# Three expert tiles of the first image beside the second image's routing

## The chip, the cores and the metric

The kernel runs on one core of a Trainium2 chip. Its metric is the device time of one execution in microseconds (us). TensorE (PE) does matmuls and transpositions, VectorE (DVE) and ScalarE (ACT) elementwise work, reductions and function tables, GpSimd (POOL) elementwise work and indirect DMA, SyncE (SP) issues DMAs. DMAs are issued from SP, ACT and POOL, each with a queue of its own.

## The reference, cut to what matters

Two images x of 128 channels and 56 x 56 pixels go through four layers, each added to its input after a group norm. This is what the change touches, and its neighbours:

```python
x = x + agent_attention(gn(x))
x = x + conv3x3(gn(x))
# layer 2: 784 tokens of 512 numbers per image (2x2 patches), 8 experts, best two per token
logits = xp @ router_w
topv, topi = top_k(softmax(logits), 2); topv = topv / sum(topv)
for e in range(8):
    val, g = split(xp @ w1[e], 2)           # 512 -> 2 x 1024
    out += gate[:, e:e+1] * ((val * sigmoid(g)) @ w2[e])    # 1024 -> 512
x = x + out
# layer 3: two mambas over the 56 pixels of each row, forward and backward, fused, layer norm
x = x + bidirectional_mamba(gn(x))
```

## The kernel before

All is float32, x stays in SBUF, and the layers follow one another.

**Attention** (`short_attention`) ends with a tail in an order written out by hand: the last attention block's closing steps are interleaved with image 0's convolution in eight parts (four groups, `left` and `right` of each), by the list `tail`, one entry ahead of each part. After the last part, ten small VectorE operations look at extremes that were gathered on the way (`bad`, `worst`), one TensorE product sums them over partitions (L871), and `wide` is set (L872): a branch at the kernel's end repeats everything with a slower attention if an exponential went out of range. The scope's memory is handed on after that.

**Convolution and routing.** `PatchExperts.route` runs image 1's convolution (a generator that yields after each of its groups) and, after its first group, `patches(0)`: group norm of image 0, tokens laid out as columns (`xq`), router products `l_ps` (L1098) and `s_ps` (L1108), the best two experts by small VectorE operations (`hots`), and the tokens turned to rows `xt` (L1142, L1144; four buffers) and written to DRAM `xd` by SP (L1145). After the convolution comes `patches(1)`, and then one routing of all 1568 tokens: products with ones and a triangle count tokens per expert (`tot`, `pre`), a scan over tokens and experts gives each token a slot, experts get as many 128-slot tiles as they need (`tiles`, `ends`), `whose` is the expert of each tile, and 28 products of one-hot masks (56 records, L1267) turn token-to-slot into slot-to-token: `inv`, copied to `whom` (token of each slot) and `share` (its gate). All of this comes in the order that the framework's scheduler picks from the program's order and its own estimate of when operands are ready.

**Experts** (`run`): 25 tiles always, and as many more as a branch (`Switch`) asks for; here 28 in all. A tile loads its expert's `w1` (4 MB, L1303) and `w2` (2 MB, L1308) on SP into two buffers each, POOL gathers 128 rows from `xd` by `whom` (L1281), TensorE transposes them (L1320), VectorE copies (`xs_c`), 16 products give `h_ps` (L1330, 32 records), ScalarE and VectorE gate them (L1333, L1334). `down` of the tile before follows: transpositions (L1343), copies, 8 products `o_ps` (L1351, 16 records), scaling, and a write to DRAM `os` on ACT's queue (L1354).

**MambaWeights** turns the mamba layer's weights: 27 loads on ACT's queue (16 of them the transposed `A`, L1498), scalings (L1471), 30 transpositions with a VectorE copy each (L141, L142) and four products (L1490). It stands after `route` in the program; its buffers are free from the end of attention, so the scheduler puts its loads at 914 to 937 us and its transpositions at 936 to 1005 us.

**Mambas** (`mamba_pair`): in fixed order. `arrive(b)` gathers and adds the expert rows of image b (`combine`, seven steps and a last one) and takes its group norm in three stages. The opening books the first block's forward way (`f`) and backward way (`b`) at steps -31 to -1 (`conv`, `silu`, `low`, `step`, `error`, `log`, `softplus`, `weigh`, `send_steps`); after each step a tuple says how many steps of image 1's `arrive` follow. `send_steps` of the first block's f copies `dtu` on SP and `dt` on ACT's queue, eight DMAs each (L1795). Then 448 units run, each a decay on ACT (L1807), a product on POOL (`dBu`, L1818) and a scan on VectorE (L1840).

Of the kernel before, what the change touches and what calls it, by code (L numbers as in the profile page):

```python
# [10 lines left out]
ALU = mybir.AluOpType  # L11
# [397 lines left out]
def short_attention(net, wide, conv):  # L409
# [20 lines left out]
    with ExitStack() as ctx:  # L430
# [337 lines left out]
        with tc.manual_schedule(engines={E.PE, E.Activation, E.DVE}):  # L768
# [55 lines left out]
            for f in fetches:  # L824
                if f:
                    f()

# [7 lines left out]
                [deviations],  # L835
# [15 lines left out]


            bad = net.small.tile([P, 4], F32, name="bad", tag="bad")
            nc.vector.memset(bad, 0.0)
            worst = net.small.tile([P, 4], F32, name="worst", tag="worst")
            aflat = asum.rearrange("t b k h -> t (b k h)")
            for n, (v, op, cmp, limit) in enumerate(
                (
                    (ends[:, 0].rearrange("p b k -> p (b k)"), ALU.max, ALU.is_gt, 1e20),
                    (ends[:, 1].rearrange("p b k -> p (b k)"), ALU.min, ALU.is_lt, 1e-30),  # L860
                    (aflat, ALU.max, ALU.is_gt, 1e30),
                    (aflat, ALU.min, ALU.is_lt, 1e-20),
                )
            ):
                size = v.shape[0]
                nc.vector.tensor_reduce(worst[:size, n : n + 1], v, AX.X, op)
                nc.vector.tensor_single_scalar(bad[:size, n : n + 1], worst[:size, n : n + 1], limit, cmp)
            total = net.small.tile([P, 1], F32, name="bad_sum", tag="bad_sum")
            nc.vector.tensor_reduce(total, bad, AX.X, ALU.add)
            w_ps = bank("w_ps")  # L870
            nc.tensor.matmul(w_ps[0:1, 0:1], full[:, 0:1], total, start=True, stop=True)  # L871
            nc.vector.tensor_single_scalar(wide, w_ps[0:1, 0:1], 0.5, ALU.is_gt)  # L872
# [130 lines left out]
TILES = 32  # L1003


class PatchExperts:

# [14 lines left out]
    def route(self, dram, wpool, conv):  # L1022
# [9 lines left out]
        with tc.tile_pool(name="l2_route", bufs=1) as one, tc.tile_pool(  # L1032
            name="l2_route_ps", bufs=2, space=PSUM
        ) as ps:
            self.fewest = -(-2 * toks // SLOTS)
            none = one.tile([SLOTS, 512], F32, name="none")
# [38 lines left out]
            nc.gpsimd.tensor_scalar(floor, count_to[:, :most], float(SLOTS), 0.0, ALU.mult, ALU.add)  # L1075

# [5 lines left out]
            per = nt // NB  # L1082

            def patches(b):
                if b == 0:
                    self.xq = wpool.tile([P, 4, 2 * self.hidden], F32, name="xq", tag="w1")
                xq = self.xq
                mr = net.group_norm(b, ps, "tr")
                for q in range(4):
                    net.normed(  # L1090
                        xq[:, q, b * tok : (b + 1) * tok].rearrange("c (h w) -> c h w", w=half), self.place(b, q), mr
                    )
                lq = one.tile([P, tok], F32, name="lq", tag="lq")
                size = tok // 2
                for i in range(2):
                    l_ps = ps.tile([P, 512], F32, name="l_ps", tag="tr")
                    for q in range(4):
                        nc.tensor.matmul(  # L1098
                            l_ps[32 * q : 32 * q + 32, :size],
                            rw[:, q, :],  # L1100
                            xq[:, q, b * tok + i * size : b * tok + (i + 1) * size],
                            start=True,
                            stop=True,
                        )
                    nc.scalar.copy(lq[:, i * size : (i + 1) * size], l_ps[:, :size])
                s_ps = ps.tile([P, 512], F32, name="s_ps", tag="tr")
# [32 lines left out]
                for t in range(b * per, (b + 1) * per):  # L1139
                    tp = ps.tile([P, 512], F32, name="xt_ps", tag="tr")  # L1140
                    for q in range(4):
                        nc.tensor.transpose(tp[:T, q * P : (q + 1) * P], xq[:, q, t * T : (t + 1) * T], net.ident)  # L1142
                    xt = one.tile([T, 512], F32, name="xt", tag="xt", bufs=4)
                    nc.scalar.copy(xt, tp[:T, :])  # L1144
                    nc.sync.dma_start(self.xd[t * T : (t + 1) * T, :], xt)  # L1145

            for _ in conv(0):
                pass
            for k, _ in enumerate(conv(1)):
                if k == 0:  # L1150
                    patches(0)
            patches(1)


            share = [one.tile([T, nt], F32, name=f"share{n}") for n in range(2)]
            nc.vector.tensor_sub(share[1], tops[1], tops[0])
            nc.scalar.activation(share[1], share[1], AF.Exp)
            nc.vector.tensor_scalar_add(share[0], share[1], 1.0)
            nc.vector.reciprocal(share[0], share[0])
            nc.vector.tensor_mul(share[1], share[1], share[0])  # L1160


            both = one.tile(shape, F32, name="both")
            nc.vector.tensor_add(both, hots[0], hots[1])
            flat = both.rearrange("t n e -> t (n e)")
            tot = ps.tile([P, 512], F32, name="tot", tag="tr")
            nc.tensor.matmul(tot[:, : nt * experts], every, flat, start=True, stop=True)
            pre = ps.tile([P, 512], F32, name="pre", tag="tr")
            nc.tensor.matmul(pre[:T, : nt * experts], before, flat, start=True, stop=True)
            by_e = one.tile([P, experts, nt], F32, name="by_e")  # L1170
            nc.vector.tensor_copy(by_e, tot[:, : nt * experts].rearrange("p (n e) -> p e n", e=experts))
            upto = one.tile([P, experts, nt], F32, name="upto")
            nc.vector.tensor_tensor_scan(
                upto.rearrange("p e n -> p (e n)"),
                step.rearrange("p e n -> p (e n)"),
                by_e.rearrange("p e n -> p (e n)"),
                0.0,
                ALU.mult,
                ALU.add,
            )  # L1180

            over = one.tile([P, experts, most], F32, name="over")
            nc.vector.tensor_tensor(
                over,
                upto[:, :, nt - 1 : nt].to_broadcast([P, experts, most]),
                floor.unsqueeze(1).to_broadcast([P, experts, most]),
                ALU.is_gt,
            )
            tiles = one.tile([P, experts], F32, name="tiles")
            nc.vector.tensor_reduce(tiles, over, AX.X, ALU.add)  # L1190
            ends = one.tile([P, experts], F32, name="ends")
            nc.vector.tensor_tensor_scan(ends, every_e(net, one, experts), tiles, 0.0, ALU.mult, ALU.add)

            more = keep.tile([1, 1], I32, name="more")
            nc.vector.tensor_scalar_add(more, ends[0:1, experts - 1 : experts], -float(self.fewest))
            self.more = more

            past = one.tile([P, TILES, experts], F32, name="past")
            nc.vector.tensor_tensor(
                past,  # L1200
                ends.unsqueeze(1).to_broadcast([P, TILES, experts]),
                count_to.unsqueeze(2).to_broadcast([P, TILES, experts]),
                ALU.is_le,
            )
            whose = one.tile([P, TILES], F32, name="whose")
            nc.vector.tensor_reduce(whose, past, AX.X, ALU.add)
            self.whose = keep.tile([P, TILES], I32, name="whose_i")
            nc.vector.tensor_scalar_min(self.whose, whose, float(experts - 1))

            nc.vector.tensor_sub(upto, upto, by_e)  # L1210
            start = one.tile([P, experts], F32, name="start")
            nc.vector.tensor_sub(start, ends, tiles)
            nc.vector.tensor_scalar_mul(start, start, float(SLOTS))
            slot = one.tile(shape, F32, name="slot")
            nc.vector.tensor_tensor(
                slot,
                pre[:T, : nt * experts].rearrange("t (n e) -> t n e", e=experts),
                upto[:T].rearrange("p e n -> p n e"),
                ALU.add,
            )  # L1220
            nc.vector.tensor_tensor(slot, slot, start[:T].unsqueeze(1).to_broadcast(shape), ALU.add)


            self.slots = []
            inv = ps.tile([P, 512], F32, name="inv", tag="tr")
            rooms = [
                wpool.tile([P, self.hidden // P, 512], F32, name="room0", tag="w2").rearrange("p j d -> p (j d)"),
# [62 lines left out]
    def run(self, wpool, work, ps):  # L1290
# [68 lines left out]
        for j in range(self.fewest):  # L1359
# [3 lines left out]
            if last is not None:  # L1363
                down(*last)
# [765 lines left out]
```

## Time and profile before

| what | us |
|---|---|
| median of 3 runs (3123.26 to 3127.08) | 3124.91 |
| the profiled execution | 3131.49 |
| its span | 3129.8 |
| attention and image 0's convolution end | 933.5 |
| image 1's convolution, TensorE | 938.5 to 982.8 |
| routing until the first expert rows are there | 982.8 to 1031.4 |
| experts, TensorE | 1031.4 to 1678.9 |
| opening of the mambas, until the first scan | 1678.9 to 1757.1 |
| mambas | 1757.1 to 3129.8 |

The profile is of one execution. TensorE is busy 2836.3 us of the span, VectorE 2229.0, ScalarE 1758.0, GpSimd 1495.6. Lines of the timeline read: start, duration, engine, line of the kernel, operation, output<-inputs, shapes, count, and in brackets the idle time before it with what released it. PE records of float32 products come in two per product.

### The profile page before, as it was taken

The numbers are of one execution on the slowest core, as the hardware profiler recorded it, in microseconds if no ns is written. First come the engines' busy times: TensorE is split into PE (matmuls) and PEld (weight loads), VectorE is DVE, ScalarE is ACT, GpSimd is POOL, SyncE is SP. The second block draws the span as 40 slices with busy tenths as digits, with TensorE's granted clock in tenths as the row PEclk, the third lists the DMA queues.
The fourth block names the chain that finished last, engine by engine and source line by source line (L and its number), as shares of the span: only waits on it lengthen the run. The fifth ranks groups of instructions, "written<-read, shape, count | busy, mean of one in ns | idle before, by whom it ended". The sixth has DMA issues, their size and how long they took to land. (4 is left out here: it accounts for less than half of the span.)

```text
span 3129.8 us, 34601 instructions
## 1 busy us (share of the span) xinstructions
PE 2836.3 (91%) x12964; PEld 1082.0 (35%) x12964; DVE 2229.0 (71%) x2033; ACT 1758.0 (56%) x2634; POOL 1495.6 (48%) x793
## 2 busy tenths in 40 slices
PE   7999999999988899999996789989899899899885
PEld 3333333332335444444443223333223333233321
DVE  5879999998886011111112689999999999999996
ACT  5778888887741011111110577776777776777764
POOL 3000100100521000000002589999999999999996
PEclk9999999999998899999997789999889998899987
DMA  1000000000011777777854553444434535444440
GB/s 54 1 1 1 1 1 1 1 1 1 1 38 53 311 308 302 301 310 292 319 194 161 104 110 77 93 92 102 90 84 86 114 81 107 90 85 91 93 101 8
DMA packets 133525, 333.64 MB, mean 107 GB/s; under 512 B 20228, under 2 KB 90724, under 8 KB 129748
## 3 DMA queue, kind: packets, MB, share of 16 engines
q1 hardware_dynamic: 111104, 303.96, 33.8%
q0 software_dynamic: 5136, 14.70, 1.4%
q10 hardware_dynamic: 17092, 12.53, 1.3%
q8 instruction: 106, 1.74, 0.2%
q14 instruction: 87, 0.71, 0.1%
HBM read 262.56 MB, written 17.20 MB: 89 GB/s over the span
## 5 line engine op out<-in xcount | busy, mean ns | idle before, releaser
L1818 POOL TENSOR_TENSOR dBu<-dtu,Bs 128x896 f32<-128x896 f32 x448 | 944.9, 2142 | 54.9 <-DVE h L1840 45.4
L1840 DVE TENSOR_TENSOR_SCAN h<-dA,dBu 128x896 f32<-128x896 f32 x448 | 879.1, 2007 | 51.3 <-ACT dA L1807 49.2
L620 ACT ACTIVATE ex<-sc 128x896 f32<-128x896 f32 (+1 forms) x700 | 602.6, 917 | 125.1 <-PE sc L617 113.8
L627 DVE TENSOR_TENSOR ex_sum<-ex_sum,ex 128x1792 f32<-128x1792 f32 (+1 forms) x238 | 492.5, 2069 | 35.3 <-ACT ex L620 21.3
L1860 PE MATMUL y<-h,both 128*64 128x448 f32 x1792 | 477.3, 635 | 13.7 <-POOL h L1846 12.6
L617 PE MATMUL sc<-q,k 32*128 32x448 f32 (+1 forms) x2800 | 403.8, 588 | 3.6 <-ACT ex L620 2.9
L1330 PE MATMUL h_ps<-w,xs_c 128*128 128x512 f32 x896 | 392.7, 596 | 11.8 <-issue 9.9
L1807 ACT ACTIVATE dA<-dt,f_A 128x448 f32<-128x448 f32 x448 | 284.4, 637 | 104.8 <-DVE h L1840 76.6
L635 PE MATMUL av<-ex,va 128*32 128x448 f32 (+1 forms) x2800 | 334.4, 552 | 0.1
L1849 DVE TENSOR_TENSOR h<-h,c_ps 128x1792 f32<-128x1792 f32 x154 | 311.3, 2022 | 26.8 <-PE c_ps L1828 12.3
L1334 DVE TENSOR_TENSOR he<-h_ps,sg 128x512 f32<-128x512 f32 x56 | 38.6, 691 | 397.7 <-PE h_ps L1330 374.9
L582 POOL TENSOR_TENSOR a_e<-a_e,a_inv 112x784 f32<-112x784 f32 x14 | 41.6, 2973 | 584.2 <-ACT ex L620 394.6
L1807 ACT ACTIVATE dA<-dt,b_A 128x448 f32<-128x448 f32 x448 | 283.7, 636 | 62.0 <-DVE h L1840 49.8
L1281 POOL DMA_INDIRECT xr<-xd,whom x28 | 28.0, 999 | 534.7 <-PE xr_ps L1320 494.7
L1846 POOL TENSOR_TENSOR h<-h,Cs 128x1792 f32<-128x1792 f32 x70 | 279.3, 3990 | 5.9 <-DVE h L1840 5.9
L1828 PE MATMUL c_ps<-low,ident 40*64 40x448 f32 x616 | 172.3, 640 | 91.5 <-DVE h L1849 69.3
L1330 PEld LDWEIGHTS h_ps<-w,xs_c 128*128 128x128 f32 x896 | 168.7, 191 | 220.3 <-issue 202.4
L1860 PEld LDWEIGHTS y<-h,both 128*64 128x64 f32 x1792 | 118.3, 152 | 320.6 <-issue 258.5
L617 PEld LDWEIGHTS sc<-q,k 32*128 32x128 f32 (+1 forms) x2800 | 137.9, 181 | 230.1 <-issue 132.5
L1351 PE MATMUL o_ps<-w,ht 128*128 128x512 f32 x448 | 198.7, 596 | 7.9 <-DMA w<-in_L_conv_w_dram 7.9
L1353 ACT ACTIVATE ot<-o_ps,share 128x512 f32<-128x512 f32 x28 | 19.2, 687 | 285.7 <-PE o_ps L1351 285.7
L1333 ACT ACTIVATE sg<-h_ps 128x512 f32<-128x512 f32 x56 | 33.4, 597 | 257.9 <-PE h_ps L1330 257.9
(333 smaller groups left out, 3067.5 us busy)
## 6 DMA issues: line engine op xcount, KB each, us to landing
w<-in_L_conv_w_dram SPq DMA_DIRECT2D x28, 4096.0 KB, 19.4
w<-in_L_conv_w_dram SPq DMA_DIRECT2D x28, 2048.0 KB, 10.2
Bs<-far SPq DMA_DIRECT2D x56, 896.0 KB, 10.7
dtu<-sp_u SPq DMA_DIRECT2D x108, 224.0 KB, 3.9
dt<-dt SPq DMA_DIRECT2D x108, 224.0 KB, 5.2
Cs<-far SPq DMA_DIRECT2D x140, 112.0 KB, 7.4
os<-ot ACTq DMA_DIRECT2D x28, 256.0 KB, 7.7
xd<-xt SPq DMA_DIRECT2D x14, 224.0 KB, 2.7
```

The lines of the kernel that those rows point to most:

```text
L617: nc.tensor.matmul(sc[:size, j, :BLK], self.m.k[rows, at : at + size], self.q[rows, :], start=True, stop=True)
L620: nc.scalar.activation(ex[:size, 2 * g : 2 * g + 2, :], sc[:size, :, :BLK], AF.Exp, scale=scale)
L627: nc.vector.tensor_add(self.total[g][:size], self.total[g][:size], ex[:size])
L635: nc.tensor.matmul(self.av[rows, :BLK], self.m.va[:size, i, rows], self.ex[i][:size, h, :], start=i == 0, stop=i == STEPS - 1,)
L1330: nc.tensor.matmul(h_ps, xc[:, q, :], w1[:, q, f0 : f0 + 512], start=q == 0, stop=q == 3)
L1351: nc.tensor.matmul(o_ps, ht[:, i, :], w2[:, i, :], start=i == 0, stop=i == nj - 1)
L1807: nc.scalar.activation(self.dA[u][:, r * BLK : (r + 1) * BLK], self.dt2[:, m, r, :], AF.Exp, scale=self.w.A[:, j, 2 * m + r : 2 * m + r + 1],)
L1818: nc.gpsimd.tensor_tensor(self.dBu[u], self.dtu2[:, m], self.B[:, j, :].unsqueeze(1).to_broadcast(shape), ALU.mult)
L1840: nc.vector.tensor_tensor_scan(hf, af, bf, 0.0, ALU.mult, ALU.add)
L1846: nc.gpsimd.tensor_tensor(h4, h4, c, ALU.mult)
L1849: nc.vector.tensor_tensor(h4, h4, c, ALU.mult)
L1860: nc.tensor.matmul(self.y[r * H : (r + 1) * H, m, :BLK], both, self.hc[j][:, m, r, :], start=False, stop=j == PAIRS - 1)
```

## The change

1. **Verdict.** The ten VectorE operations (`judge`) and the product with `wide` (`verdict`) become entries six and eight of the attention's `tail`.
2. **Early tiles.** After `patches(0)`, `first_tiles` routes image 0's tokens alone and numbers the tiles that its tokens fill entirely (`ALU.is_ge` on `full`); the first three, `EARLY`, get their own `whose_0`, `whom_0`, `share_0`. `ahead` issues their loads and gathers and keeps their TensorE work as a list of 21 stages. `patches(1)` and the routing of all tokens then run with TensorE and ScalarE in the order of the program, and `go(n)` puts n stages between their steps; while `held` is a list, the sigmoid with its multiplication is kept back until `patches(1)` is through. The global routing numbers the full tiles of image 0 first, over 2 x 8 ends in place of 8.
3. **Memory.** The pools of weights, work and PSUM are open from the convolution on. `xq` and the masks lie in `room`, which the mambas' weights take over afterwards; `xt` has two buffers in place of four; masks of one image at a time.
4. **MambaWeights** loads into a pool that opens after `route`, and its outputs lie in `room`.
5. **Opening.** The tuple changes, and the first block's `dt` DMAs go from ACT's queue to POOL's.

The core of the diff:

```diff
             tail = [
...
-                [deviations],
+                [deviations, judge],
+                [],
+                [verdict],
             ]
...
             def patches(b):
-                mr = net.group_norm(b, ps, "tr")
+                go = self.go if b == 1 else lambda n: None
+                got = []
+                go(2)
+                for stage in net.norm_stages(b, ps, "o", got.append):
+                    fetch = stage()
+                    if fetch:
+                        fetch()
+                        go(1)
+                mr = got[0]
...
                     nc.scalar.copy(lq[:, i * size : (i + 1) * size], l_ps[:, :size])
+                go(1)
...
-                    xt = one.tile([T, 512], F32, name="xt", tag="xt", bufs=4)
+                    xt = one.tile([T, 512], F32, name="xt", tag="xt", bufs=2)
                     nc.scalar.copy(xt, tp[:T, :])
                     nc.sync.dma_start(self.xd[t * T : (t + 1) * T, :], xt)
+                shares(some)
+                if b == 1:
+                    held, self.held = self.held, None
+                    for stage in held:
+                        stage()
+                    go(1)
...
             for k, _ in enumerate(conv(1)):
                 if k == 0:
                     patches(0)
-            patches(1)
+                    first_tiles()
+                    self.ahead()
+            with tc.manual_schedule(engines={mybir.EngineType.PE, mybir.EngineType.Activation}):
+                patches(1)
...
+                self.go(2)
...
+                for n in range(2):
+                    at_n = one.tile([T, nt], F32, name=f"at{n}")
+                    split(hots[n], slot, slice(0, nt), at_n)
...
+                    for b in range(NB):
+                        self.go((0, 2, 1, 1)[2 * n + b])
+                        turned(
...
+                self.go(len(self.stages))
...
         def expert(j):
-            return bass.ds(nc.sync.value_load(self.whose[0:1, j : j + 1], ...), 1)
+            whose = self.whose_0 if j < EARLY else self.whose
+            return bass.ds(nc.sync.value_load(whose[0:1, j : j + 1], ...), 1)
...
+        def ahead():
+            self.stages, self.held = [], []
+            for j in range(EARLY):
+                e = expert(j)
+                self.stages += step(j, e, up_weights(e), gather(j))
...
-        for j in range(self.fewest):
+        for j in range(EARLY, self.fewest):
...
-                for to, src, queue in (..., (self.dt2, self.dt, nc.sync if m is None else nc.scalar)):
+                for to, src, queue in (..., (self.dt2, self.dt, nc.sync if m is None else nc.gpsimd)):
...
-                for _ in range((0, 0, 0, 0, 2, 1, 2, 1, 2, 0, 0, 0, 0, 0, 1, 1, 1)[step - first] if step - first < 17 else 1):
+                for _ in range((0, 0, 0, 2, 0, 1, 1, 0, 1, 1, 1, 1, 0, 1, 1, 1)[step - first] if step - first < 16 else 1):
...
-                    experts.route(dram, wpool, convolved)
-                    wts = MambaWeights(net, one, nat, bank)
-                with tc.tile_pool(name="l2_work", bufs=2, reuse_waits="tile") as work, tc.tile_pool(
-                    name="l2_ps", bufs=2, space=PSUM
-                ) as ps:
-                    experts.run(wpool, work, ps)
+                    experts.begin(wpool, work, ps)
+                    room = one.tile([P, 4 * experts.tok], F32, name="room", tag="room")
+                    experts.route(dram, work, ps, room, convolved)
+                    with tc.tile_pool(name="l3_nat", bufs=2) as nat:
+                        wts = MambaWeights(net, one, nat, bank)
+                    experts.run()
```

`step` is `up` and the `down` of the tile before it as a list of stages: the transposition, four half products (each pair followed by its gating), the transposition of `down`, two halves of its product. The 21 stages are those of tile 0 (5), tile 1 (8) and tile 2 (8). In order, `patches(1)` runs six of them, two follow the slots, four lie between the masks, and nine come after the last product of `inv`.

## Prediction

> **What bounds the kernel now.** I read the table of stages first. Attention (to 894 us) and the mambas (from 1757 us) are touched only at their ends, so the middle decides. There TensorE is nearly idle-free while experts run, and half starved before them:
>
> ```profile
> 982.80:1031.36 48.56, 30.68 (x159) 24.05 (x157) 28.37 (x113) 6.14 (x14) 5.46 (x6) 0.68 0.44 166
> ```
> ```profile
> 1094.80:1117.35 22.55, 22.16 (x61) 10.37 (x60) 2.67 (x4) 2.47 (x4) 0.99 (x1) 1.00 0.77 302
> ```
>
> After the stage and its length the columns are busy time of PE, PEld, DVE, ACT and POOL, granted clock, DMA share and GB/s. One expert tile takes 22.55 us, 22.16 of them TensorE's: nothing but TensorE work removed or filled in shortens that stage. The routing stage ahead of it has 48.6 us with 30.7 busy at clock 0.68. The timeline shows the serial end of it:
>
> ```profile
> 1011.26 12.18 PE L1267 MATMUL inv<-room 112*128 112x64 f32 x56 [5.18 <-DVE tile_f L1242]
> ...
> 1023.48 0.19 DVE L1276 CAST whom<-inv 128x32 int32<-128x32 f32 x1 [8.46 <-PE inv L1267]
> ...
> 1023.96 1.14 POOL L1281 DMA_INDIRECT xr<-xd,whom  x1 [39.06 <-DVE share L1278]
> ...
> 1031.36 0.88 PE L1320 MATMUL xr_ps<-ident,xr 128*128 128x128 f32 x3 [7.92 <-DMA xr<-xd,whom]
> ```
> ```profile
> 1094.81 0.60 PE L1320 MATMUL xr_ps<-ident,xr 128*128 128x128 f32 x4
> ```
>
> No expert can start before `whom` (1023.5) and its gather (1031.4). Tile 3, the first that the changed kernel runs in the old way, starts its transposes at 1094.81. The size of the middle's gain is how much earlier that row comes. The page's DMA issues bear on the rivals:
>
> ```profile
> w<-in_L_conv_w_dram SPq DMA_DIRECT2D x28, 4096.0 KB, 19.4
> w<-in_L_conv_w_dram SPq DMA_DIRECT2D x28, 2048.0 KB, 10.2
> ```
>
> In steady state SP issues the 2 MB and 0.6 us later the 4 MB; they land after 10.2 and 19.4 us, so the second one moves in the 9.8 us after the first: on SP's queue a transfer waits for what was issued before it.
>
> **Part 1, verdict.** Judge and verdict move into the attention's tail. Now the next stage waits for them:
>
> ```profile
> 935.68 0.15 DVE L872 TENSOR_SCALAR wide<-w_ps 1x1 int32<-1x1 f32 x1 [0.37 <-PE w_ps L871]
> 935.76 0.12 POOL L933 MEMSET scratch<- 128x16 f32 x1 [3.35 <-PE w_ps L871]
> ```
>
> The last statistics end at 933.5, the first plane is normalized at 935.92: **-2.4 us**. The ten small DVE operations (1.9 us) then lie beside conv matmuls that run to 929.8; without that cover they cost at most their 1.9.
>
> **Part 2, three tiles beside the routing.** TensorE is the bound from the end of image 1's conv (982.8) on, so I add up its work until tile 3.
> Start: 982.8 - 2.4. `first_tiles` puts 28 small matmuls into the conv stream, which is packed (13.73 us of conv records without a gap up to 982.8). The 56 like them took 12.18 us, 0.217 each, at granted clock 0.50; the projection of 112 columns (L674) ran at 0.13 each at clock 1.00. Bounds 3.6 and 6.1; I take 3.6, since TensorE is warm there. Conv ends at 984.0.
> Work: three tiles, 67.7; routing of image 1: l_ps 3.6, s_ps 1.6, xt 4.2, totals and norms 1.5, inv 56 x 0.13 = 7.3 (bound 12.2). Sum 18.2. Without a wait tile 3 starts at 984.0 + 67.7 + 18.2 = 1069.9, 25 us earlier than now.
> Waits: (a) tile 0's transposes stand ahead of image 1's norm in TensorE's order and need `whom_0`. Image 0's choice is made at 966.8; the chain from there to the last mask takes 13.6 us now (1001.4 to 1015.0); with image 0 alone its masks halve, but conv's DVE work stands between, so 13.6 stays, plus 1.5 for the last products: 981.9. Issue 1.1 and 7.3 us to land (the row above) give 990.3, less the 2.4 of part 1: 987.9. TensorE waits 3.9. (b) The copy `xs_c` after a transposition is uncovered for two tiles: 2. (c) `xt` has 2 buffers instead of 4. A write of it lands in 2.7 us and its copy takes 0.6, so the seven go in pairs of 3.3: about 3 late. ScalarE's held sigmoids stand behind these copies, with a table load of 1.28, and tile 1's products need the banks that they free: 3 more, 6 together. (d) `inv` waits for masks: 2. Sum 13.9.
> Tile 3 at 1083.8 instead of 1094.8: **-11.0 us, part 1 included**. Bounds: -25 (no wait) and +12 (the queue of the second rival, with the upper bounds of the small products).
>
> **Part 3, the mambas' weights** move behind the routing, into the stage where TensorE has 0.4 us free per tile. 30 transpositions at 0.15 (four take 0.60 at L1320) and 8 records of L1490 at 0.19 are 6.0 us, with no cover any more; their DVE work (50 operations of 0.28) has it, 2.7 of 22.55 being busy. Their 27 loads, 0.3 to 0.8 us of issuing each on ACT's queue, and two Exp now share ACT's order and the DMA engines with the experts (ACT is busy 2.5 of 22.55). Where they stand now they cost nothing that comes back: ACT's conv copies wait for them 5.5 and 3.1 us, but the conv records behind run packed. In the idle queues each 2 KB load of `A` landed in 2.3 us; beside weights I take 2 us of waiting (bounds 0 and 25). **+8.0 us.**
> The Trainium skill (DMA: Bandwidth & Descriptors, "Rules for kernel authors") speaks against the place: a strided last dimension becomes one descriptor per element, and its section on queues says that an engine alternates between queues at packet boundaries. By that the 16 `A` loads are 8192 descriptors that take turns with 32 KB ones, and the wait would lie near the upper bound, 25, and the sum at +14. No row of before has such loads beside weights.
>
> **Part 4, the opening.** The first scan now starts behind a chain:
>
> ```profile
> 1747.90 8.01 PE L1690 MATMUL conv_ps<-pad,b_conv_t 128*128 128x448 f32 x16
> ...
> 1750.23 0.64 ACT L1807 ACTIVATE dA<-dt,f_A 128x448 f32<-128x448 f32 x1 [3.60 <-DMA dtu<-sp_u]
> ...
> 1755.75 0.28 PE L116 MATMUL gn_ps<-gn_q,group 128*128 128x1 f32 x2
> ...
> 1756.26 0.20 ACT L67 ACTIVATE ir_t<-ir_v 128x1 f32<-128x1 f32 x1 [5.39 <-DVE ir_v L66]
> 1756.37 0.62 ACT L1807 ACTIVATE dA<-dt,f_A 128x448 f32<-128x448 f32 x1
> ...
> 1757.09 2.02 DVE L1840 TENSOR_TENSOR_SCAN h<-dA,dBu 128x896 f32<-128x896 f32 x1 [0.86 <-ACT dA L1807]
> ```
>
> The second half of the first decay stands on ACT behind image 1's root, this behind a product that TensorE runs after 8.0 us of conv. In the new order the root's product comes one step ahead of that conv, so this wait goes: the decay could end at 1751.5. What is late next is dBu on POOL (1750.58 + 2.13). POOL now issues eight `dt` transfers first, 0.8 each by its one direct issue (L1043): the four ahead of each memset push dBu to about 1753. Against that `step` no longer waits for two more combines (1730.97 would be 1728.2), -2.8, and ACT loses 2.6 us of issuing ahead of the second softplus. First scan at 1750 to 1751; way b's silu with its two table loads still stands between the first decays, so I take **-6 us**, bounds 0 and -10. From there on POOL is busy 478 and DVE 468 of every 500 us, so the shift stays to the end.
> The skill's first-byte figures (same page, "Latency and other measured facts") give POOL's queue 0.4 us more per transfer. The sum with that would be 0.4 higher.
>
> **Sum.** -11.0 + 8.0 - 6 = -9.0. The profiled execution took 3131.49 (span 3129.8), 6.6 above the median of the runs: applied to it 3122.5, to the median 3124.9 - 9.0 = **3116 us**. 0.2%, 6.2 us, is about what a measurement of this kernel can tell from no change.
>
> **Rivals.**
> *The waits fit.* The go() quotas cover waits (a) to (d) by half and the loads by luck of order: -7 and -2 more, -18: 3107. For it: ACT is busy 6.1 and DVE 28.4 of that stage's 48.6 us, and TensorE's clock stays up. Against it: its order is fixed, so one late operand stops all.
> *The queue on SP (slower).* Tile 0's 6 MB are issued as soon as `whose_0` is read, at about 971 (966.8 and the 4.2 us that `whose_i` now takes from 1001.4 to 1005.6). With two `xt` buffers the last writes of image 0's rows leave at about 975. If they stand behind, they land at 971.5 + 9.8 + 10.2 = 991.5, the gather at 1000 instead of 990: +9. The same again when tile 2's 4 MB, freed by tile 0's last product, go ahead of image 1's seven writes: the third copy waits up to 9.8 instead of 2.7, +7. Together +16: +7, 3132. It decides once it costs more than 9.0; above 15.2 it shows as slower.
> *The loads stop an engine.* An Exp of `A`, or a transposition of way b, stands in its engine's order and its bytes crawl behind weights: 10 to 20 more, +1 to +11, 3131. TensorE then idles between tiles 3 and 6.
> *It doesn't overlap.* Tile 0 comes so late that the routing simply starts after it; this is the queue's case with the same price and is counted there.
>
> **Numbers.** Forecast 0.44, waits fit 0.16, queue 0.22, loads 0.18. Faster: most of the first (0.38), all of the second, 0.01 of the loads: 0.55. Slower: 0.17 of the queue, 0.11 of the loads: 0.28. Same: the rest, 0.17. The forecast's own range is 3109 to 3122. The range over the cases goes down to the fitted waits with all loads hidden, 3100, and up to queue and loads in part together, 3139.
>
> **What would show it.** Right: `wide` written before the last conv statistics; xr_ps of tile 0 at 985 to 992; tile 3's at 1078 to 1089; transpositions L141 between experts with gaps under 1 us; first scan 70 to 74 us after the last expert product. Wrong: SP's xd writes landing after more than 8 us (queue); TensorE idle for over 5 us between experts before the Switch with ACT or a DMA as releaser (loads); a first scan still 78 us after that product (1678.9 to 1757.1 now).

## The result and the profile after

The changed kernel runs in 3123.76 us (median of 20), the kernel before, beside it on the same chip, in 3123.67 (median of 20). One run of the changed kernel was slow, 4028.81 us at a granted clock of 0.64, and is left out of the ratio of the mean times, 0.9994, 95% interval [0.9987, 1.0002]: -1.9 us, between -4.1 and +0.6. No difference can be told. The forecast was -9.0.

The two profiled executions (spans 3129.8 and 3125.7) can't be subtracted as they stand. Attention, which the change leaves alone but for its tail, ends 3.19 us earlier in the second (last `y_ps` at 901.88 and 898.69), 2.4 of it there already at 60 us. So I count from the end of that product:

| us from the end of attention's last y_ps | before | changed | difference |
|---|---|---|---|
| image 1's convolution starts | 36.63 | 36.08 | -0.6 |
| image 1's convolution ends | 80.92 | 85.91 | +5.0 |
| tile 0, xr_ps | 129.48 | 91.26 | -38.2 |
| tile 3, xr_ps | 192.93 | 190.70 | -2.2 |
| tile 4, xr_ps | 215.48 | 217.97 | +2.5 |
| last expert product ends | 777.01 | 780.01 | +3.0 |
| first scan | 855.21 | 854.07 | -1.1 |

Tile 0 starts 38 us earlier, and three tiles later nearly all of that is gone. The timeline of the changed kernel shows the start (PE's line names the gather that it waited for) and then the stretch in which it is lost:

```profile
989.95 1.11 PE L1465 MATMUL xr_ps<-ident,xr 128*128 128x128 f32 x4 [5.35 <-DMA xr<-xd,whom]
```
```profile
1010.64 0.33 SPq L1443 DMA_DIRECT2D w<-in_L_conv_w_dram  x1
...
1012.42 1.07 ACT L1165 COPY xt<-xt_ps 112x512 f32<-112x512 f32 x2 [4.92 <-PE xt_ps L1163]
...
1013.03 18.18 SPq L1166 DMA_DIRECT2D xd<-xt  x7
...
1014.92 0.28 DVE L1330 TENSOR_TENSOR both<-hot,hot 112x112 f32<-112x112 f32 x1
1024.39 1.15 ACT L1165 COPY xt<-xt_ps 112x512 f32<-112x512 f32 x2 [10.91 <-DMA xd<-xt]
...
1025.03 1.96 PE L1163 MATMUL xt_ps<-ident,room 128*112 128x128 f32 x8 [10.84 <-ACT xt L1165]
...
1028.90 1.06 PE L1465 MATMUL xr_ps<-ident,xr 128*128 128x128 f32 x4
...
1035.07 1.22 PE L1475 MATMUL h_ps<-w,xs_c 128*128 128x512 f32 x1 [3.44 <-DVE he L1484]
```

Read it from the bottom of the wait. TensorE stands 10.84 us for ACT's copy `xt`; ACT stands 10.91 for a write of `xd`, since two buffers are full; and the writes were issued at 1013.03, 2.4 us behind tile 2's `w1` of 4 MB. VectorE has chosen the experts by 1015.2 and waits too. Behind it tile 1's products wait 3.44 us for gates that were held back.

The table of stages (length, busy PE, PEld, DVE, ACT, POOL, granted clock, DMA share, GB/s), from the end of the convolution to the transposes of tile 1, from these to those of tile 2 and of tile 3, then tile 3 and tile 4:

```profile
984.60:1028.90 44.30, 26.07 (x100) 14.05 (x100) 9.29 (x31) 5.12 (x11) 3.29 (x4) 0.79 0.84 324
1028.90:1065.76 36.86, 32.86 (x122) 18.97 (x121) 21.37 (x74) 4.85 (x8) 2.22 (x3) 0.84 0.19 53
1065.76:1089.39 23.63, 22.55 (x63) 10.50 (x62) 2.67 (x4) 2.36 (x4) 1.85 (x2) 1.00 0.83 312
1089.39:1116.66 27.27, 27.27 (x99) 13.56 (x98) 12.12 (x46) 2.47 (x4) 1.00 (x1) 1.00 0.64 251
1116.66:1139.20 22.54, 22.15 (x61) 10.36 (x60) 2.67 (x4) 2.47 (x4) 1.00 (x1) 1.00 0.76 303
```

TensorE is idle for 18 of 44 us in the first. In tile 3's stage, with the mambas' weights in it, it is busy all the time, and the stage is 4.7 us longer than tile 4's (27.27 against 22.54). The attention's tail and the opening:

```profile
928.83 0.13 DVE L853 TENSOR_SCALAR wide<-w_ps 1x1 int32<-1x1 f32 x1
```
```profile
1738.97 7.85 SPq L1995 DMA_DIRECT2D dtu<-sp_u  x8
...
1743.61 0.16 DVE L66 TENSOR_SCALAR ir_v<-gn_ps 128x1 f32<-128x1 f32 x1 [0.54 <-PE gn_ps L116]
1743.81 0.20 ACT L67 ACTIVATE ir_t<-ir_v 128x1 f32<-128x1 f32 x1 [2.79 <-DVE ir_v L66]
...
1749.50 0.64 ACT L2007 ACTIVATE dA<-dt,f_A 128x448 f32<-128x448 f32 x1 [5.25 <-DMA dt<-dt]
...
1750.66 2.07 POOL L2018 TENSOR_TENSOR dBu<-dtu,Bs 128x896 f32<-128x896 f32 x1 [6.35 <-DMA dtu<-sp_u]
...
1752.76 2.02 DVE L2040 TENSOR_TENSOR_SCAN h<-dA,dBu 128x896 f32<-128x896 f32 x1 [7.68 <-POOL dBu L2018]
```

`wide` no longer stands between the layers, and ACT takes image 1's root at 1743.81, ahead of the decays. They now wait for the `dt` transfers, and the scan waits longer, for `dBu`, which POOL starts when the `dtu` copies have landed. Counted from the last expert product, these copies are issued 4.2 us sooner than in the kernel before (60.28 against 64.44), and yet `dBu` starts no sooner (71.96 against 71.69).

### The profile page after: what moved, and what is told of

It reads as the page before. It is cut to its first block, busy times and chain, and to the rows that moved or that the text cites. A ratio compares the mean times of both kernels' runs of the same rounds, so it can differ in the third digit from the quotient of the medians.

```text
span 3125.7 us, 34650 instructions
## 1 busy us (share of the span) xinstructions
PE 2831.0 (91%) x12996; PEld 1075.4 (34%) x12996; DVE 2242.2 (72%) x2096; ACT 1758.6 (56%) x2635; POOL 1492.7 (48%) x804
## 5 line engine op out<-in xcount | busy, mean ns | idle before, releaser
L2060 PE MATMUL y<-h,weights 128*64 128x448 f32 x1792 | 472.9, 629 | 11.9 <-POOL h L2046 10.8
L1475 PE MATMUL h_ps<-w,xs_c 128*128 128x512 f32 x896 | 400.1, 602 | 16.1 <-issue 9.9
L2060 PEld LDWEIGHTS y<-h,weights 128*64 128x64 f32 x1792 | 117.1, 151 | 318.5 <-issue 252.8
L1890 PE MATMUL conv_ps<-pad,weights 128*128 128x448 f32 x448 | 185.3, 561 | 3.6 <-issue 2.4
## 6 DMA issues: line engine op xcount, KB each, us to landing
w<-in_L_conv_w_dram SPq DMA_DIRECT2D x28, 2048.0 KB, 10.4
```

What stands on the lines that cost most here:

```text
L1475: nc.tensor.matmul(has["h"][:, n, :], has["xc"][:, q, :], w1[:, q, f0 : f0 + 512], start=q == 0, stop=q == 3)
L2060: nc.tensor.matmul(self.y[r * H : (r + 1) * H, m, :BLK], both, self.hc[j][:, m, r, :], start=False, stop=j == PAIRS - 1)
```

## The experiments

My first theory was the prediction's rival, in its second half: the writes of image 1's rows stand behind `w1` on SP's queue. Its rivals were the two buffers as such, a gain that is lost again in the expert stage, and a whole that is only the opening's. Line numbers in profiles of variants are their own.

**The writes on POOL's queue (e1_writes_pool).**

```diff
-                    nc.sync.dma_start(self.xd[t * T : (t + 1) * T, :], xt)
+                    (nc.gpsimd if b else nc.sync).dma_start(self.xd[t * T : (t + 1) * T, :], xt)
```

> The changed kernel with one line edited: the seven writes of the second image's rows (xd<-xt) are issued by POOL instead of SP; the first image's stay on SP. Theory (the queue on SP): in the changed kernel TensorE stood 10.84 us at 1025.03 because these writes were issued behind tile 2's 4 MB w1 (1010.64) and only two xt buffers exist. Away from SP's queue a write lands in about 2.5 us, so the xt copies run in pairs of some 3.5 us: tile 1's xr_ps moves from 1028.9 to about 1021.5, tile 3's from 1089.4 to 1082, and the whole by -6 to -8 us against the changed kernel, 0.9970 to 0.9977 of the kernel before. Rival A (the two buffers alone, whatever the queue): the wait stays over 7 us, tile 1 not before 1026, time within 2 us of the changed kernel (0.999). Rival B (the time goes further back, into the expert stage and the Switch): tile 3 comes 7 us earlier, but the last expert product stays within 2 us of 1678.7.

3131.12 us, 1.0015 of the kernel before [1.0003, 1.0027]. The wait is the same on another queue:

```profile
1017.62 0.33 SPq L1443 DMA_DIRECT2D w<-in_L_conv_w_dram  x1
...
1020.28 1.19 POOL L1166 DMA_DIRECT2D xd<-xt  x2 [24.87 <-ACT xt L1165]
1031.50 1.15 ACT L1165 COPY xt<-xt_ps 112x512 f32<-112x512 f32 x2 [11.03 <-DMA xd<-xt]
...
1032.14 1.95 PE L1163 MATMUL xt_ps<-ident,room 128*112 128x128 f32 x8 [10.96 <-ACT xt L1165]
```

10.96 instead of 10.84: that another queue would free the writes was wrong. The packets in the trace tell why, and that there are two mechanisms with one price:

| | w1's 128 packets of 32 KB | first two writes' packets |
|---|---|---|
| changed kernel (SP's queue) | 1011.61 to 1023.38 | all from 1022.60 on, when an engine's share of w1 is through |
| e1 (POOL's queue) | 1018.60 to 1031.05 | from 1024.13 to 1031.61, among them, about one for one |

A 32 KB packet takes 1.21 us, one of the writes 0.08 to 0.16. The Trainium skill (DMA: Bandwidth & Descriptors, "Rules for kernel authors") says that spreading DMAs over SP, ACT and GpSimd does not help bandwidth, since all run on the same engines and interleave; this run agrees, and shows that it does not help a small write's wait either.

Tile 1 comes 39.67 us after tile 0 instead of 38.95, and the last expert product ends at 779.97, as in the changed kernel (780.01). The rest of the +6 is elsewhere: the profiled execution ended attention 7.5 us later, with a granted clock of 0.73 between 160 and 185 us (1.00 in the changed kernel's), and its first scan comes 76.8 behind the last expert product instead of 74.1 (77.2 in e9 below, which writes from POOL too). That part is not explained.

**w1 later in the program (e2_w1_late).** Tile 2's `up_weights` and `down_weights` called behind the loop of writes.

> The changed kernel with tile 2's two weight loads (w1, w2) requested in the program's order behind the seven writes of the second image's rows, instead of ahead; all stay on SP's queue, with two xt buffers. Theory (the queue on SP): the same gain as with the writes on POOL, tile 1's xr_ps at about 1021.5, tile 3's at 1082, -6 to -8 us against the changed kernel; w1 then leaves at about 1020 instead of 1010.6, lands 20 us later, at 1040, ahead of its use at about 1058, so nothing is lost. Rival A (two buffers alone): no change, within 2 us. Rival C (the late load costs what the early writes win): tile 1 early, but tile 2's first h_ps waits for w1, and tile 3 stays at 1087 to 1091.

3125.41 us, 0.9998 [0.9986, 1.0011]. The edit did not do what it says: SP's order is the scheduler's, and it issued `w1` at 1014.50, after two of the writes. Those landed at once (a wait of 1.90 us), the other five stood behind `w1`, and the wait moved: 13.52 us, ended at 1031.01. A hint for the theory, no test of it.

**The opening alone, and all but the opening (e3_opening_alone, e4_no_opening).**

```diff
-for _ in range((0, 0, 0, 0, 2, 1, 2, 1, 2, 0, 0, 0, 0, 0, 1, 1, 1)[step - first] if step - first < 17 else 1):
+for _ in range((0, 0, 0, 2, 0, 1, 1, 0, 1, 1, 1, 1, 0, 1, 1, 1)[step - first] if step - first < 16 else 1):
...
-(self.dt2, self.dt, nc.sync if m is None else nc.scalar)
+(self.dt2, self.dt, nc.sync if m is None else nc.gpsimd)
```

e3 is the kernel before with this, e4 the changed kernel without it.

> The kernel before with part 4 alone: the new tuple that spreads the second image's arrival over the opening's steps, and the split dt transfers on POOL instead of ACT. Theory (the opening is what is left of the change): last expert product unmoved at 1678.9 within 0.3, first scan 74 us after it instead of 78.2, whole -4 us, 0.9987 of the kernel before (interval 0.998 to 0.9995). Rival (the opening's gain in the changed kernel comes from the earlier parts, such as weights already turned or room in memory): first scan still 77 to 78 us after the last expert product, time within 1 us of before.

> The changed kernel without part 4: the tuple and the queue of the dt transfers as in the kernel before, the early tiles, the verdict and the moved weights kept. Theory: parts 1 to 3 together are worth nothing at the end: tile 3's xr_ps at 1089.4, tile 4's at 1116.7, last expert product at 1678.7, first scan 78 us after it at 1757, and the time that of the kernel before, ratio 0.9990 to 1.0010. Rival (the early tiles give something that shows only at the end): 0.9985 or less, with a first scan before 1755. Rival (they cost and the opening hides it): over 1.0010.

e3: 3120.36 us, 0.9980 [0.9968, 0.9991]; first scan 73.61 behind the last expert product (78.20 before). e4: 3132.30 us, 1.0012 [1.0002, 1.0022]; 77.29, and the last expert product at 780.52 against 777.01. So the opening gives 6 us (3 to 10), parts 1 to 3 together cost 4 (1 to 7), and the changed kernel is their sum (-2.5 by these two, -1.9 measured). That e4 would be even was wrong, though its interval begins near even. The rows agree: the last expert product ends at 779.7 to 780.6 in the six profiles that have the early tiles, two buffers and `w1` ahead of most writes (changed, e1, e2, e4, e9, e10), at 777.0 and 776.6 without early tiles (before, e3). The even time is two effects that cancel.

**The verdict alone (e5_verdict_alone).** The kernel before with part 1.

> The kernel before with part 1 alone (judge and verdict inside the attention's tail). One look at the rows, counted from the end of the attention's last y_ps product, since the attention itself ends 1 to 4 us earlier or later from run to run. Before: conv of the second image ends 80.92 behind it, tile 3's xr_ps 192.93; changed kernel: 85.91 and 190.70. Forecast's theory: part 1 is worth 2.4 us or more, conv ends at 78.5, tile 3 at 190.5. Rival (what looked like -3.85 is the attention's own shift): the first normalized plane moves from 34.04 to about 33.4 and conv ends at 80.3, -0.7; then first_tiles puts 5.7 us into the conv stream of the changed kernel, not 3.6.

In the one profiled run image 1's convolution starts at 34.47 (before 36.63; 37.03 in e3, which has that stage too) and ends at 79.47 (80.92), tile 3 at 191.72 (192.93). The verdict is worth 2.2 to 2.6 us where it stands and 1.2 at tile 3. In the changed kernel only 0.6 is left at the start, as VectorE reaches `bad_sum` late there and TensorE waits for it:

```profile
925.82 0.19 PE L852 MATMUL w_ps<-bad_sum,full 128*1 128x1 f32 x2 [0.93 <-DVE bad_sum L847]
```

Loads and a scaling of `A` stand in its way: counted from the last `y_ps`, ACT takes the root of image 1's norm at 23.02 in the changed kernel, right behind an `A` load, and at 22.03 in e5; VectorE then has a scaling of `A` (1.03 us) ahead of the last check, and `bad_sum` comes at 26.92 instead of 25.52.

**w1 strictly behind the writes (e6_w1_behind), four buffers (e7_xt4), both (e8_w1_behind_xt4).**

```diff
-with tc.manual_schedule(engines={mybir.EngineType.PE, mybir.EngineType.Activation}):
+with tc.manual_schedule(engines={mybir.EngineType.PE, mybir.EngineType.Activation, mybir.EngineType.SP}):
...
                 shares(some)
                 if b == 1:
+                    self.late_w1()
```
```diff
-                    xt = one.tile([T, 512], F32, name="xt", tag="xt", bufs=2)
+                    if t % 2 and b:
+                        xt = work.tile([SLOTS, 512], F32, name="xt", tag="ot")[:T, :]
+                    else:
+                        xt = one.tile([T, 512], F32, name="xt", tag="xt", bufs=2)
```

`late_w1` requests tile 2's two loads, which `ahead` then leaves out. e6 is the first, e7 the second, e8 both.

> The changed kernel, tile 2's w1 and w2 loads requested behind the seven writes of the second image's rows and SP's order held as written, so that w1 can't be issued until the last write is. Theory, as mended by the POOL run (the writes' packets wait in the DMA engines for the 32 KB packets of w1, on SP's queue behind all of them, on POOL's one packet per turn): without w1 in flight a write lands in 2 to 2.5 us, the seven copies take about 10 us in pairs, TensorE never waits 10 us; from the end of the attention's last product tile 1's xr_ps comes at 122 to 123 instead of 130.2, tile 3's at 183, the last expert product at 772.5 instead of 780.0; time -7 us against the changed kernel, about 0.997 of the kernel before. Rival (w1 then comes too late): tile 2's h_ps wait for w1 and tile 3's xr_ps stays at 189 to 191. Rival (the two buffers alone): tile 1 over 128.

> The changed kernel with four xt buffers for the second image (two of them in room that the expert outputs leave free), SP's queue and its order as they are, w1 in front. One look. Theory: the first four copies run at once, the fifth waits until the writes land behind w1's last packet, at about 124 behind the attention's last product; tile 1's xr_ps at 126 to 127 instead of 130.2: -3 to -4, the wait for the DMA still 7 to 8 us long. Rival (buffers alone are the cause): the wait falls under 3 us and tile 1 comes at 119 to 121.

> Both edits: w1 and w2 of tile 2 behind the writes with SP's order held, and four xt buffers. Theory: copies at 0.6 us each almost without a wait, tile 1's xr_ps at 118 to 119 behind the attention's last product (changed kernel 130.2), tile 3's at 179 to 180, last expert product at 769, that is 8 us ahead of the kernel before (777.0) and 11 ahead of the changed kernel; with the opening's 4 about -12 us in all, 0.996 of the kernel before. Rival (something else is late next, the choice's DVE chain and the held sigmoids): tile 1 early, tile 3 no earlier than with the order alone, 183.

| | changed | e6 | e7 | e8 |
|---|---|---|---|---|
| longest wait of ACT for a write, us | 10.91 | 1.90 | 9.79 | 0.59 |
| tile 1, xr_ps | 130.21 | 121.30 | 127.84 | 117.80 |
| tile 3, xr_ps | 190.70 | 181.15 | 187.25 | 177.16 |
| last expert product | 780.01 | 769.57 | 776.42 | 766.42 |
| of the kernel before | 0.9994 | 0.9975 [0.9965, 0.9986] | one run | 0.9957 [0.9940, 0.9974] |

The timeline of e6, and below it of e8:

```profile
1013.89 9.15 SPq L1166 DMA_DIRECT2D xd<-xt  x7
...
1016.25 0.59 ACT L1165 COPY xt<-xt_ps 112x512 f32<-112x512 f32 x1 [1.90 <-DMA xd<-xt]
...
1020.73 1.06 PE L1469 MATMUL xr_ps<-ident,xr 128*128 128x128 f32 x4
...
1023.29 0.36 SPq L1444 DMA_DIRECT2D w<-in_L_conv_w_dram  x1
```
```profile
1016.19 5.11 SPq L1169 DMA_DIRECT2D xd<-xt  x7
...
1018.57 0.58 ACT L1168 COPY xt<-xt_ps 112x512 f32<-112x512 f32 x1 [0.59 <-DMA xd<-xt]
...
1019.69 0.60 PE L1472 MATMUL xr_ps<-ident,xr 128*128 128x128 f32 x4
...
1021.55 0.36 SPq L1447 DMA_DIRECT2D w<-in_L_conv_w_dram  x1
...
1023.89 8.83 PE L1482 MATMUL h_ps<-w,xs_c 128*128 128x512 f32 x16 [2.42 <-DVE he L1491]
```

With nothing in flight the writes pass in 9 us in pairs, or 5 with four buffers, and `w1`, issued 12 or 8 us later, makes no product wait. The order alone returns 9.6 us at tile 3, the buffers alone 3.5, both 13.5, and what tile 3 wins reaches the last product (-10.4 and -13.6), so nothing is lost in the expert stage. Buffers alone help less than predicted (tile 1 at 127.84, not 126 to 127): the fifth copy still waits for a write that stands behind `w1`. e8 beats both kernels: about -13 us against the one before.

**Own queue, small packets (e9_pool_pieces), SP's queue, small packets (e10_sp_pieces).** Tile 2's `w1` in four transfers `w1[:, :, f]` of 512 columns, whose packets are 2 KB; e9 with the writes on POOL as in e1.

> The changed kernel with the second image's writes on POOL's queue, as in the first run, and tile 2's w1 loaded in four transfers whose packets are 2 KB instead of 32 KB (512 columns at a time); w1 still in front of the writes. One look. Theory (on a queue of their own the writes get one packet per turn, and a turn is as long as w1's packet): with turns of 0.085 us instead of 1.21 a write lands in 3 to 4 us though w1 is in flight, the wait of 10.96 us for xt goes to 1 to 2, tile 1's xr_ps comes at 122 to 124 behind the attention's last product (130.4 with 32 KB packets), tile 3's at 183 to 185. Rival (the DMA engines simply finish the 4 MB first, or share by bytes): the wait stays over 7 us, tile 1 over 127.

> The changed kernel, all on SP's queue and in its order, with tile 2's w1 in 2 KB packets as in the run beside it. One look. Theory (within one queue the packets go in the order of issue, whatever their size): the writes still come behind the whole of w1, TensorE waits 9 to 12 us for xt, tile 1's xr_ps at 129 to 132. Rival (the packet's size is all that matters, on any queue): tile 1 at 122 to 124.

e10 is as expected: 11.97 us, tile 1 at 131.21. e9 is not: tile 1 at 129.82, in two waits instead of one.

```profile
1014.34 1.19 POOL L1166 DMA_DIRECT2D xd<-xt  x2 [25.01 <-ACT xt L1165]
1021.08 0.59 ACT L1165 COPY xt<-xt_ps 112x512 f32<-112x512 f32 x1 [6.55 <-DMA xd<-xt]
...
1028.02 1.24 ACT L1165 COPY xt<-xt_ps 112x512 f32<-112x512 f32 x2 [5.42 <-DMA xd<-xt]
```

Once they run, two writes' packets are through in 2.6 us (1018.88 to 1021.51; 7.5 in e1), so turns are shorter with small packets. But the first of them starts 4.5 us after the issue (3.9 in e1; 1.1 for the writes at 1032.38 of e1, with `w1` landed), and with two buffers that is paid twice. What holds them back these 4 us is open. The second two writes of e9 are through at 1028.12, `w1` at 1028.17. On either queue and with either packet tile 1 stays at 129.8 to 131.2; the order moves it, and less so the number of buffers.

**Gates at once (e11_no_hold), weights behind the experts (e12_weights_after),** both from e8: `self.held` is None from the start; `MambaWeights` stands behind `experts.run()`.

> The kernel with w1 behind the writes and four xt buffers (e8), without the held sigmoids: ScalarE gates each pair of products at once instead of behind the second image's xt copies. Theory (the held gates cost the 2.42 us that TensorE waits for he behind tile 1's transposes, but the table loads of 1.28 us that come instead stand in the norm's chain): two or three more loads ahead of l_ps, l_ps 2 to 4 us later, tile 1's h_ps right behind its xr_ps; tile 3's xr_ps within 2 us of 177.2, time within 0.1% of e8 (0.9957 of the kernel before). Rival (the hold is pure cost): tile 3 at 173 to 175. Rival (the loads pile up): tile 3 at 181 or later.

> The kernel e8 with the mambas' weights turned behind the experts instead of behind the routing, so that their transposes leave tile 3's stage. Theory (part 3 costs the 4.7 us that tile 3's stage takes over 22.55, and nothing else): tile 3 to tile 4 in 22.55 us, last expert product at 761.7 instead of 766.4; what is won there comes back only if the opening's 74 us have room: I expect them not to, since loads, scaling and transposes then stand in front of the second conv, 5 to 15 us more from the last expert product to the first scan (74 in e8), time 0 to +10 us against e8. Rival (the opening's TensorE is idle enough): first scan still 74 to 75 us behind the last expert product, -4 to -5 us against e8, 0.994 of the kernel before.

e11: 3112.97 us, 0.9956 [0.9942, 0.9970]; tile 3 at 179.32, last expert product 768.65. Without the hold four table loads of 1.28 us stand ahead of the writes' copies, in e8 none; that is worth 2.2 us at tile 3, and no time that can be told. e12: 3120.30 us, 0.9981 [0.9972, 0.9991], 7 us behind e8. The stages of e12, tile 3 and the opening:

```profile
1078.57:1101.10 22.53, 22.18 (x61) 10.36 (x60) 2.67 (x4) 2.47 (x4) 1.00 (x1) 1.00 0.77 303
1663.01:1749.09 86.08, 51.06 (x155) 27.61 (x154) 44.42 (x150) 18.43 (x31) 35.66 (x39) 0.68 0.52 130
```

Part 3 costs tile 3 its 4.7 us and nothing more; in the opening the same work costs 11.9 (86.08 against 74.22).

## Why the prediction was half right

The range over all cases, 3100 to 3139, held the time; the forecast's own, 3109 to 3122, did not, and no change had a chance of 0.17. The forecast, -9.0, was 7 off (-1.9), and the largest step, -11.0 at tile 3, failed. In the rows tile 3 misses by +8.8, part 3 by -3.3, the rest of the experts by +0.5 and the opening by +1.9, which turns -9.0 into the first scan's -1.1. That it did not end worse is partly luck: part 3 had been priced too high.

- **Part 1, -2.4.** Right where it is made (e5: -2.2 to -2.6). That its VectorE work lies under conv matmuls for nothing was not: in the whole change `bad_sum` comes late and 1.6 go back.
- **`first_tiles`, 3.6 in a packed conv stream.** The stretch grew from 44.29 to 49.83, 5.5. The 28 records cost 3.4, about as priced; totals (0.7) and waits of TensorE, most of them for masks (about 1), were not counted. With part 1's loss the convolution ends 5.0 later instead of 1.2: 3.8 of the miss.
- **Waits (a) to (d), 13.9 in all.** TensorE is idle 23.3 of the 104.8 us between the convolution's end and tile 3 (busy 26.07, 32.86 and 22.55 in the three stages). (a) is 5.35 instead of 3.9, though its chain counts the gather's issue twice (7.24 from issue to transposes here, 8.4 in the sum). (c), 6, is the step that failed: 10.84, and 3.44 for the held gates. I had priced `xt`'s pairs by writes that land in 2.7 us in empty queues, and set the 4 MB in front of them aside as a rival of 0.22. TensorE's own work was 81.5 instead of 85.9, so tile 3 is 5.0 late here. The 85.9 was added up wrongly: 67.7 holds three `down`s, and two stand ahead of tile 3's transposes, which in the kernel before come 63.45 behind tile 0's. That is 8.2 too much (7.03 of `o_ps` and twice 0.60 of `he_ps`), and products that ran slower behind the waits took about half of that back (16 records of `h_ps` 10.03 us at 1035.07, 7.08 at 1046.45). Without that slip the forecast for tile 3 would have been about -19, and further off.
- Together 8.8: tile 3 at -2.2 instead of -11.0. e6 and e8 give it back: -11.8 and -15.8.
- **Part 3, +8.0.** 4.7 measured. The 6.0 of TensorE work was 5.1 (27.27 busy against 22.15), 0.4 of it in what had been gaps, and the 2 us of waiting none: the 16 `A` loads did not move (910.9 to 927.0 now), the other 11 left at 1057.8 to 1062.8, between two tiles' weights. The rival of the loads fell with it; what the skill's rule on strided loads would cost beside weights, no run shows.
- **Part 4, -6.** -4.1 in the two profiles, 6 (3 to 10) by e3. The root's wait went as said, and what is late next is `dBu`, as said. But the 2.8 us that `step` wins do not reach it, since it waits for `dtu`: in e3 the first of these copies lands 7.2 us after its issue (3.2 in the kernel before), at 1745.78, right behind the last of the `Cs` copies that SP issued ahead of it (1745.23). It is the wait of part 2 once more; no run moves these copies. Way b's silu comes behind the first scan (1755.44).
- **The rival of SP's queue.** Its second half came true in size (+7 predicted for the third copy, and 10.84 seen), and so did its sign, a write that lands after more than 8 us. Its cause holds by half: on SP's queue the writes do stand behind `w1`, but on POOL's the wait is as long (e1), so it is the load in flight and not the queue that costs. Its first half did not come true: image 0's writes were all issued by 970.9, before tile 0's `w1` at 973.3.

## What to carry to other kernels

A transfer that is issued early for a distant use can hold up small ones that are issued after it: here 4 MB in front cost a critical chain 10.8 us, and putting the load behind the seven writes gave 9.6 us back at tile 3. Before moving a load up, list the short transfers in a critical chain that will be issued while it is in flight, and try the load behind them (another queue or smaller packets did not help here). Where a program's order is the scheduler's, look at the issue times in the trace before believing that an edit moved a DMA. And an even result can be a loss and a gain: take the parts singly, counted from a point that the change doesn't touch.

## What the runs showed of the hardware

- A 224 KB write behind a 4 MB load came through after 11 us on the load's own queue (all packets behind) and on POOL's (interleaved) alike; with nothing in flight its waiting copy stood 1.9 us.
- Packets that POOL issued started 1.1 us after the issue with idle DMA engines, 3.9 and 4.5 with the load in flight, whatever its packet size.
- In e6, after 5.39 us of idleness the first 8 records of h_ps took 5.92 us, the next 8 took 3.68: this wait of TensorE cost more than its length.
